# A graph attention layer with a mixture of experts: the first destination terms behind another block's softmax, flags made during the features, one scan across partitions, rows normalised on ScalarE

## The chip, the cores and the metric

The kernel runs on one core of one Trainium2 chip. The metric is device time in microseconds (us) of one execution; the median of ten runs is given. A profile is one execution recorded by the hardware profiler. The engines are TensorE (PE; its weight loads PEld), VectorE (DVE), ScalarE (ACT), GpSimd (POOL) and SyncE (SP, which here only issues DMAs). Each works through its own instructions in order.

## The reference, cut to what matters

30,000 nodes with 256 features, 510,000 edges sorted by destination, 8 relations, 4 heads of 64. A graph attention layer with a residual is followed by a feed-forward layer with a shared network and 4 experts, of which each node takes 2.

```python
# _layernorm(x) = (x - mean) / sqrt(var + 1e-5)
feat_all = jnp.einsum('ni,rhid->rnhd', inputs, conv_weights)      # inputs = _layernorm(x)
feat_src_e = feat_all[edge_type, edge_src]
feat_dst_e = feat_all[edge_type, edge_dst]
el = jnp.sum(feat_src_e * attn_l[edge_type], axis=-1)
er = jnp.sum(feat_dst_e * attn_r[edge_type], axis=-1)
e = jax.nn.leaky_relu(el + er, negative_slope=0.2)
m = jax.ops.segment_max(e, edge_dst, num_segments=N_NODES)
ex = jnp.exp(e - m[edge_dst])
alpha = ex / jax.ops.segment_sum(ex, edge_dst, num_segments=N_NODES)[edge_dst]
h = jax.ops.segment_sum(alpha[..., None] * feat_src_e, edge_dst, num_segments=N_NODES)
x = x + h.reshape(N_NODES, 256) + h_bias
x = x + ffn(_layernorm(x))     # shared + gated top 2 of 4 experts, three layers each
```

## The kernel before

**Stage 1, the features** (0 to about 1740 us). For each of 235 tiles of 128 nodes, `group` multiplies the normalised rows with all relations' weights in five groups of columns (L305), `store` writes the rows of features `feat` to memory, 1040 bytes for each node and relation: four heads of 64 and a 65th element, the source term `el`. `dest_pieces` writes the destination terms as three bf16 pieces, `erp_d`. Beside this, one step at a time (`aside`), run three generators: `edge_records`, `places` and `expert_weights`. `places` takes the edges in batches of 12 blocks, loads their records (`fetch`, tile `rcb`), and makes for each block a row of data `rk_d` of 128 partitions x `WR` words: gather indices (`WI`), the node of each edge (`WD`), marks of duplicates (`WA`), penalties of -1e30 where a new destination begins (`WP`), running minima of these from the left and from the right (`W1`: "no boundary so far", "no boundary after") and one-hot relations (`WT`). Where a generator says `yield`, its next instructions come at a later place of the feature loop. Last, `first_rows` gathers the first edge row of each block already in this stage into staging buffers (`fr`, three of them) and writes them to `stage`: the gathers are GpSimd's, the writes SP's.

**Stage 2, the blocks** (to about 6590 us). The edges are cut into 252 blocks of at most 2048 (128 partitions x `U` = 16 edges), with a 253rd of 18 a partition. Edges of a partition follow each other, so a destination's run of edges may go on from one partition to the next. The steps of block t:

- `load`: SP loads `rk`, `dr`, `erp`, `xt`. `gather`: one row from `stage` (SP), 15 rows by GpSimd's indirect DMA (L933) into a ring of four blocks (`ft`).
- `dest_select` (VectorE, L970) makes one-hot rows `ohT`; `dest_expand` (TensorE, L987, four matmuls for a quarter of the block) brings the destination terms of each edge into PSUM (`pe`, two buffers); `dest_pick` (VectorE, L998 and L1000) picks those of its relation into `e`. Four quarters each.
- `flags` (ScalarE, L951 to L955) copies the penalties to each head and the two end values into `ends`; `flags_across` (TensorE L962, ScalarE L964) turns the ends so that the 128 partitions stand in a row.
- `scores` (VectorE, L1027 to L1034) adds the gathered source terms, applies the leaky slope, and scans running maxima from the left and the right within each partition, `fb`. `turn_ends` (TensorE, L1040, L1041), `across` (VectorE, L1047 and L1048, two scans over 128 partitions), `turn_back` (TensorE, L1055, L1056) carry the maxima across partitions. `softmax` (VectorE, L1062 to L1065 and `exchange`) subtracts the maximum; `exps` (ScalarE, L1071, L1072) takes the exponential.
- `onehot` (ScalarE, L1010, L1011) makes one-hot columns of the destinations; `weigh` (VectorE, L1079) multiplies the gathered rows by the weights, and `sums` (TensorE, L1086) adds them by destination in one PSUM tile `po`; `finish` (VectorE, L1104 to L1107) divides (`den`, `ho`).
- `residual_sum` adds the residual. Four blocks make a group of 512 nodes for `Experts`: 22 steps (`spread`, `scale`, `turn`, `gates`, the layers, `last`), one taken from `todo` in each chunk.

The order on every engine is the order of the program, written out by hand: an iteration t has six chunks c, and each holds pieces of several blocks: block t's scores and softmax, t-1's weighing and sums, t+1's and t+2's destination terms, t+1's gathers, t+2's loads. In chunk 5 `softmax(t)` and `exps(t)` are followed on VectorE by `weigh(t, 0)` and `finish(t - 1)`; in chunk 0 of the next iteration come `weigh`, the first `dest_pick` and `residual_sum`. After the blocks come loops that run only where the input does not fit the blocks' limits; here they run zero times.

Of the kernel before, what the change touches and what calls it, by code (L numbers as in the profile page):

```python
# [10 lines left out]
F32 = mybir.dt.float32  # L11
# [34 lines left out]
WI, WD, WA, WP, W1, WT, WR = 0, U, 2 * U, 3 * U, 4 * U + 1, 6 * U + 3, 6 * U + 3 + U * 4  # L46
# [7 lines left out]
def kernel(  # L54
# [47 lines left out]
    stage = dram.tile([NBLK * P, H * HW], F32, name="stage")  # L102
    exc_d = dram.tile([P], F32, name="exc_d")
# [70 lines left out]
    NPEN = 3  # L174
    pens = []
    for i in range(NPEN + 1):
        f = wf.tile([P, H, U if i < NPEN else UL], F32, name=f"penf{i}")
        b = wf.tile([P, H, U if i < NPEN else UL], F32, name=f"penb{i}")
        nc.gpsimd.memset(f, -BIG)
        nc.gpsimd.memset(b, -BIG)  # L180
        pens.append((f, b))
    carry = []
    for i in range(2):
        cf = wf.tile([H, P + 1], F32, name=f"carf{i}")
        cb = wf.tile([H, P + 1], F32, name=f"carb{i}")
        nc.gpsimd.memset(cf, -BIG)
        nc.gpsimd.memset(cb, -BIG)
        carry.append((cf, cb))
# [33 lines left out]
    with ExitStack() as cx:  # L222
# [268 lines left out]
        def places(cl):  # L491
# [31 lines left out]
            yield  # L523
            done = None
            for k, (b0, n) in enumerate(batches):
# [33 lines left out]
                pen = kp.tile([P, GB, UW], F32, name="penk")[:, :n]  # L559
                nc.vector.tensor_scalar_mul(pen, rc[:, :, :, 3], -BIG)  # L560
                yield
                nc.gpsimd.tensor_copy(of[:, :, WP:WP + UW], pen)
                d16 = kp.tile([P, GB, U], I16, name="d16k")[:, :n]
                nc.gpsimd.tensor_copy(d16, rc[:, :, :U, 1])
                a1 = kp.tile([P, GB, UW], F32, name="a1k")[:, :n]
                a2 = kp.tile([P, GB, UW], F32, name="a2k")[:, :n]
# [7 lines left out]
                nc.gpsimd.tensor_copy(of[:, :, W1 + UW:W1 + 2 * UW], a2)  # L574
                yield
# [7 lines left out]
                def done(o=o, d16=d16, b0=b0, n=n):  # L583
                    nc.sync.dma_start(rk_d[b0:b0 + n].rearrange("b p w -> p b w"), o)
                    nc.sync.dma_start(dk_d[b0 * CAP:(b0 + n) * CAP].rearrange("(b p u) -> p b u", p=P, u=U), d16)
# [18 lines left out]
        def first_rows():  # L604

            n, kept = 4, []
            fp = cl.enter_context(tc.tile_pool(name="first", bufs=3))

            def keep(b0, m, fr):
                nc.sync.dma_start(stage[b0 * P:(b0 + m) * P, :].rearrange("(b p) f -> p b f", p=P), fr[:, :m])  # L610
            for b0 in range(0, NBLK, n):
                m = min(n, NBLK - b0)
                fr = fp.tile([P, n, H * HW], F32, name="fr")
                for b in range(m):
                    nc.gpsimd.indirect_dma_start(  # L615
                        out=fr[:, b], out_offset=None, in_=feat[0:BT * P * R, :],
                        in_offset=bass.IndirectOffsetOnAxis(ap=lowc[:, b0 + b:b0 + b + 1], axis=0))
                    if b == n // 2 and kept:
                        keep(*kept.pop())
                    count["sent"] += 1  # L620
                    yield
                kept.append((b0, m, fr))
            while kept:
                keep(*kept.pop(0))
# [77 lines left out]
    class Experts:  # L702
# [22 lines left out]
        def spread(self):  # L725
            self.rs = self.pool.tile([P, T], F32, name="c_rs")
            nc.scalar.activation(self.rs[:M, :self.n], self.mv[:M, :self.n, 1], AF.Sqrt, bias=eps[:M])

        def scale(self, j):
            if j == 0:  # L730
                nc.vector.reciprocal(self.rs[:M, :self.n], self.rs[:M, :self.n])
                self.xn = self.pool.tile([P, T, D], F32, name="c_xn")
            for t in range(j, min(j + 2, self.n)):
                nc.vector.tensor_scalar(self.xn[:M, t, :], self.x1[:M, t, :], self.mv[:M, t, 0:1],
                                        self.rs[:M, t:t + 1], op0=ALU.subtract, op1=ALU.mult)
# [126 lines left out]
    with ExitStack() as cx:  # L862
# [17 lines left out]
        flat = "p h u -> p (h u)"  # L880
        blk = {}

        class Block:


            def __init__(self, t):
                self.u = U if t < NBLK else UL
                self.sc = [-(-self.u * c // NCH) for c in range(NCH + 1)]
                self.dw = -(-self.u * P // 48) * 16
                self.dc = [-(-self.u * c // 4) for c in range(5)]  # L890
                at = t % RING * U
                self.ft = ring[:, at:at + self.u]
                self.own = t < NBLK
                self.pens = pens[t % NPEN if t < NBLK else NPEN]

        def load(t):
# [3 lines left out]
            if s.own:  # L900
# [7 lines left out]
                s.pen = rf[:, WP:WP + U + 1]  # L908
# [28 lines left out]
        def flags(t):  # L937


            s = blk[t]  # L940
            n = s.u
            s.penf, s.penb = s.pens
            if not s.own:
                s.pen = wk.tile([P, UL + 1], F32, name="pen", bufs=1)[:, :n + 1]
                nc.vector.tensor_scalar_mul(s.pen, s.rc[:, :, 3], -BIG)
                s.a12 = wk.tile([P, 2, UL], F32, name="a12", bufs=1)
                nc.vector.tensor_tensor_scan(s.a12[:, 0], s.pen[:, :n], s.pen[:, :n], 0.0, ALU.min, ALU.min)
                nc.vector.tensor_tensor_scan(s.a12[:, 1, ::-1], s.pen[:, n:0:-1], s.pen[:, n:0:-1], 0.0,
                                             ALU.min, ALU.min)
            mid = s.pen[:, None, 1:n].to_broadcast([P, H, n - 1])  # L950
            nc.scalar.copy(s.penf[:, :, 1:], mid)  # L951
            nc.scalar.copy(s.penb[:, :, :n - 1], mid)
            ends = wk.tile([P, 2, H], F32, name="ends")
            nc.scalar.copy(ends[:, 0, :], s.a12[:, 0, n - 1:n].to_broadcast([P, H]))
            nc.scalar.copy(ends[:, 1, :], s.a12[:, 1, 0:1].to_broadcast([P, H]))  # L955
            s.ends = ends

        def flags_across(t):
            s = blk[t]
            pn = ps_p.tile([H, 2, P], F32, name="pn", tag="sm")  # L960
            for i in range(2):
                nc.tensor.transpose(pn[:, i, :], s.ends[:, i, :], ident)  # L962
            s.through = wk.tile([H, 2, P], F32, name="through")
            nc.scalar.copy(s.through, pn)  # L964
# [26 lines left out]
        def dest_pick(t, c):  # L991

            s = blk[t]
            if c == 0:
                s.e = wk.tile([P, H * UL], F32, name="e")[:, :H * s.u].rearrange("p (h u) -> p h u", h=H)
# [28 lines left out]
        def scores(t):  # L1024

            s = blk[t]
            nc.vector.tensor_add(s.e, s.e, s.ft[:, :, :, HD].rearrange("p u h -> p h u"))  # L1027
            nc.vector.scalar_tensor_tensor(s.e, s.e, SLOPE, s.e, op0=ALU.mult, op1=ALU.max)
            exchange(s, s.e)
            s.fb = wk.tile([P, 2, H * UL], F32, name="fb")[:, :, :H * s.u].rearrange("p i (h u) -> p i h u", h=H)  # L1030
            s.f, s.b = s.fb[:, 0], s.fb[:, 1]
            e, f, b = s.e.rearrange(flat), s.f.rearrange(flat), s.b.rearrange(flat)
            nc.vector.tensor_tensor_scan(f, s.penf.rearrange(flat), e, -BIG, ALU.add, ALU.max)
            nc.vector.tensor_tensor_scan(b[:, ::-1], s.penb.rearrange(flat)[:, ::-1], e[:, ::-1], -BIG,  # L1034
                                         ALU.add, ALU.max)

        def turn_ends(t):
            s = blk[t]
            s.t1 = ps_p.tile([H, 2, P], F32, name="t1", tag="sm")
            nc.tensor.transpose(s.t1[:, 0, :], s.f[:, :, s.u - 1], ident)  # L1040
            nc.tensor.transpose(s.t1[:, 1, :], s.b[:, :, 0], ident)  # L1041

        def across(t):

            s = blk[t]
            cf, cb = carry[t % 2]
            nc.vector.tensor_tensor_scan(cf[:, 1:], s.through[:, 0, :], s.t1[:, 0, :], -BIG, ALU.add, ALU.max)  # L1047
            nc.vector.tensor_tensor_scan(cb[:, P - 1::-1], s.through[:, 1, ::-1], s.t1[:, 1, ::-1], -BIG,  # L1048
                                         ALU.add, ALU.max)

        def turn_back(t):
# [3 lines left out]
            nc.tensor.transpose(s.t2[:, 0, :], cf[:, :P], ident[:H, :H])  # L1055
            nc.tensor.transpose(s.t2[:, 1, :], cb[:, 1:], ident[:H, :H])  # L1056

        def softmax(t):
# [4 lines left out]
            nc.vector.tensor_max(c, c, s.fb)  # L1063
            nc.vector.tensor_max(s.f, c[:, 0], c[:, 1])
            nc.vector.tensor_sub(s.e, s.e, s.f)  # L1065
# [58 lines left out]
        with tc.manual_schedule():  # L1124
            for t in range(-2, NBLK + 12):
# [3 lines left out]
                for c in range(NCH):  # L1129
# [14 lines left out]
                    if c == 5:  # L1144
                        at(softmax, t)
                        at(exps, t)
                    if c < NCH - 1:
                        at(weigh, t - 1, c + 1)
                    if c < 4:
# [5 lines left out]
                    if c == 4:  # L1155
                        at(dest_select, t + 2)
# [4 lines left out]
                    if c == 5:  # L1161
                        at(weigh, t, 0)
                        at(dest_expand, t + 2, 0)
# [241 lines left out]
```

## Time and profile before

| what | us |
|---|---|
| median of 10 runs | 6654.76 (6643.41 to 6667.78) |
| profiled execution | 6660.21 |
| its span, first to last instruction | 6658.5 |
| first gather of a block | 1743.25 |
| TensorE busy, 0 to 1700 us | 1684.30 |
| TensorE, VectorE, ScalarE, GpSimd busy, 4000 to 5000 us | 879.95, 893.69, 612.94, 742.72 |
| mean granted TensorE clock, 0 to 1700 and 4000 to 5000 us | 1.00 and 0.96 of full speed |
| DMA share, 4000 to 5000 us | 0.56, 159 GB/s |

How the profile is read: a line of the groups gives the program line, the engine, the operation, `out<-in` by tile names, the partitions x elements of output and input, the count; then busy time in us and the mean of one in ns; then the idle time of that engine just before these instructions and what ended most of it. "issue" is idle time in which the profile shows nothing waited for. A line of the timeline gives the start, the duration, engine, line and operation, and in brackets the idle time before it with its releaser. An instruction that does not depend on the one before it may start some 0.08 us before that one's end is recorded, so start-to-start distances are shorter than durations.

### The profile page before, as it was taken

The numbers are of one execution on the slowest core, as the hardware profiler recorded it, in microseconds if no ns is written. First come the engines' busy times: TensorE is split into PE (matmuls) and PEld (weight loads), VectorE is DVE, ScalarE is ACT, GpSimd is POOL, SyncE is SP. The second block draws the span as 40 slices with busy tenths as digits, with TensorE's granted clock in tenths as the row PEclk, the third lists the DMA queues.
The fourth block names the chain that finished last, engine by engine and source line by source line (L and its number), as shares of the span: only waits on it lengthen the run. The fifth ranks groups of instructions, "written<-read, shape, count | busy, mean of one in ns | idle before, by whom it ended". The sixth has DMA issues, their size and how long they took to land. (4 is left out here: it accounts for less than half of the span.)

```text
span 6658.5 us, 96556 instructions
## 1 busy us (share of the span) xinstructions
PE 5998.4 (90%) x25254; PEld 3850.4 (58%) x25255; DVE 5351.3 (80%) x13882; ACT 3427.4 (51%) x9511; POOL 4070.3 (61%) x4327
## 2 busy tenths in 40 slices
PE   9999999999788888888888888888888888888888
PEld 5555555555456555565655656556656655656555
DVE  5555677644589998998899998889888888888996
ACT  2222222222365666666666666666566666566664
POOL 1111111266677777777777777777777777777773
PEclk9999999999899999999999999999999999999999
DMA  6666777799755555555555555555555555555552
GB/s 228 227 208 188 233 233 233 236 343 353 241 153 167 163 159 160 159 161 167 160 162 157 159 165 160 157 159 157 160 162 160 158 157 156 159 162 158 159 160 66
DMA packets 761457, 1209.52 MB, mean 182 GB/s; under 512 B 241638, under 2 KB 599789, under 8 KB 730685
## 3 DMA queue, kind: packets, MB, share of 16 engines
q1 hardware_dynamic: 565453, 663.56, 30.8%
q0 software_dynamic: 194400, 539.40, 29.5%
q8 instruction: 206, 3.38, 0.2%
q14 instruction: 358, 2.93, 0.1%
q10 hardware_dynamic: 1040, 0.26, 0.0%
HBM read 818.57 MB, written 384.23 MB: 181 GB/s over the span
## 5 line engine op out<-in xcount | busy, mean ns | idle before, releaser
L933 POOL DMA_INDIRECT ft<-feat,rk x3798 | 3606.6, 950 | 1227.5 <-issue 435.9
L1086 PE MATMUL po<-ft,oh 128*128 128x260 f32 x8100 | 2227.6, 410 | 154.5 <-DVE ho L1107 140.9
L1086 PEld LDWEIGHTS po<-ft,oh 128*128 128x128 f32 x8100 | 1520.5, 202 | 420.4 <-ACT ends L955 145.5
L305 PE MATMUL ps<-w,xT 128*128 128x448 f32 (+1 forms) x4700 | 1709.5, 519 | 10.1 <-DVE xT L294 8.4
L1079 DVE TENSOR_TENSOR ft<-ft,p 128x768 f32<-128x768 f32 x1518 | 1289.1, 849 | 182.2 <-ACT ft L1072 182.2
L1010 ACT ACTIVATE oh<-icol,rk 128x128 f32<-128x128 f32 x4032 | 1329.1, 390 | 0.0
L305 PEld LDWEIGHTS ps<-w,xT 128*128 128x128 f32 x4700 | 876.4, 191 | 699.0 <-issue 607.6
L307 ACT COPY fo<-ps 128x448 f32<-128x448 f32 (+1 forms) x711 | 377.9, 533 | 1081.4 <-PE ps L305 979.2
L1011 ACT ACTIVATE oh<-oh 128x384 f32<-128x384 f32 x1518 | 740.2, 488 | 48.1
L987 PEld LDWEIGHTS <-ohT 128*128 128x128 bf16 x4050 | 391.0, 158 | 403.5 <-issue 309.2
L1000 DVE TENSOR_REDUCE e<-ere 128x16 f32<-128x384 f32 (+1 forms) x1012 | 561.4, 555 | 34.7
L998 DVE TENSOR_TENSOR ere<-pe,rk 128x384 f32<-128x384 f32 x1008 | 551.1, 547 | 1.3 <-PE pe L987 1.3
L798 PE MATMUL ph<-xT,v 128*128 128x512 f32 (+1 forms) x1024 | 484.3, 596 | 1.1 <-ACT h L799 0.7
L987 PE MATMUL pe<-erp,ohT 128*128 128x96 bf16 x4050 | 434.5, 232 | 26.2 <-DVE ohT L970 20.7
L1071 ACT ACTIVATE p<-e 128x64 f32<-128x64 f32 (+1 forms) x253 | 71.1, 281 | 745.2 <-DVE e L1022 734.2
L307 DVE COPY fo<-ps 128x448 f32<-128x448 f32 (+1 forms) x464 | 242.7, 527 | 215.2 <-PE ps L305 209.6
L294 DVE COPY xT<-ptr 128x256 f32<-128x256 f32 x229 | 97.3, 425 | 370.2 <-PE ptr L292 368.0
L615 POOL DMA_INDIRECT fr<-feat,lowc x252 | 239.5, 950 | 169.1 <-DMA stage<-fr 69.7
L970 DVE TENSOR_SCALAR ohT<-dr,rowid 128x2064 bf16<-128x2064 int16 (+1 forms) x253 | 324.1, 1281 | 3.3 <-DMA feat<-fo 2.9
L274 POOL TENSOR_TENSOR xb<-xg,hb 128x1024 f32<-128x1024 f32 (+1 forms) x59 | 142.1, 2408 | 283.1 <-DMA xg<-in_x_dram 143.9
L851 PE MATMUL pf<-w,h 128*128 128x256 f32 x506 | 170.6, 420 | 145.2 <-ACT wT L844 111.8
L853 PE MATMUL pf<-v,a 128*128 128x256 f32 x1012 | 281.2, 403 | 0.0
(206 smaller groups left out, 6763.6 us busy)
## 6 DMA issues: line engine op xcount, KB each, us to landing
feat<-fo SPq DMA_DIRECT2D x234, 1040.0 KB
dr<-dk_d SPq DMA_DIRECT2D x252, 516.0 KB
ft<-feat,rk POOLq DMA_INDIRECT x3798
stage<-fr SPq DMA_DIRECT2D x63, 520.0 KB
ft<-stage SPq DMA_DIRECT2D x252, 130.0 KB
xt<-xb_d SPq DMA_DIRECT2D x253, 128.0 KB
out_dram<-og SPq DMA_DIRECT2D x253, 128.0 KB
xb_d<-xb SPq DMA_DIRECT2D x58, 512.0 KB
```

Of the source, the lines that this page charges most:

```text
L305: nc.tensor.matmul(ps, t["xT"][:, k, :], w[:, k, c0:c1], start=k == 0, stop=k == 1)
L307: eng(t["fo"][:, h0:h1, :HD], ps[:, :n].rearrange("p (a d) -> p a d", d=HD))
L798: nc.tensor.matmul(ps[:, :self.w], lhs, rhs, start=i == 0, stop=i == len(pairs) - 1)
L933: nc.gpsimd.indirect_dma_start(out=s.ft[:, u].rearrange("p h d -> p (h d)"), out_offset=None, in_=feat[:, :], in_offset=bass.IndirectOffse ...
L970: nc.vector.tensor_scalar(ohT[:, :3 * s.dw].rearrange("n (i e) -> n i e", i=3), s.dr[:, :, :s.dw], rowid[:, t:t + 1], None, op0=ALU.is_equal)
L987: nc.tensor.matmul(pe[:, u - u0].rearrange("p f r -> p (f r)"), s.ov[:, u, :], s.erp.rearrange("n h k r -> n (h k r)"), start=True, stop=True)
L998: nc.vector.tensor_mul(ere, s.pe[:, :u1 - u0], s.th[:, u0:u1, None, :].to_broadcast([P, u1 - u0, H * 3, R]))
L1000: nc.vector.tensor_reduce(s.e[:, :, u0:u1].rearrange("p h u -> p u h"), ere.rearrange("p u (h k) r -> p u h (k r)", h=H), AX.X, ALU.add)
L1010: nc.scalar.activation(s.oh[:, u, :], icol, AF.Abs, bias=s.nd[:, u:u + 1])
L1011: nc.scalar.activation(s.oh[:, u0:u1], s.oh[:, u0:u1], AF.Relu, bias=1.0, scale=-1.0)
L1079: nc.vector.tensor_mul(fc, fc, pc[:, :, None].to_broadcast([P, (u1 - u0) * H, HD]))
L1086: nc.tensor.matmul(s.po.rearrange("n h d -> n (h d)"), s.oh[:, u, :], s.ft[:, u].rearrange("p h d -> p (h d)"), start=u == 0, stop=u == s. ...
```

## The change

- **First destination terms.** In chunk 4 `dest_select(t + 2)` now stands ahead of the last `weigh`, and `dest_expand(t + 2, 0)` moves from chunk 5 into chunk 4. `dest_pick(t + 2, 0)` moves from chunk 0 of the next iteration to chunk 5, behind `softmax(t)` and `exps(t)`. `e` gets a third buffer.
- **Flags across partitions.** `places` makes the penalties per direction (`WP` is now 2 x `U` words, so `WR` grows from 163 to 178), and turns the end values of 12 blocks at once on TensorE (a transpose, and a product with `turned`, the matrix that reverses the partitions) into `thr_d`. In stage 2 `load` brings a block's 8 rows of it (`through`, three buffers); `flags` becomes one copy, and `flags_across` stays for the last block alone.
- **One scan.** Both directions stand in 8 rows, the right-hand one reversed by `turned`; `across` has one scan and a reversed copy instead of two scans. `turn_ends` and `turn_back` have as many matmuls as before, and `fb` becomes two fixed buffers with zeros between, cleared at the start.
- **Rows of the experts' layer norm.** ScalarE scales by 1/sigma and adds -mean/sigma, which one new small VectorE operation makes.
- **Stage 1.** `places` waits six steps instead of one after its first `fetch`; three of its tiles have one buffer instead of two; `first_rows` takes three rows a staging buffer instead of four.

```diff
-WI, WD, WA, WP, W1, WT, WR = 0, U, 2 * U, 3 * U, 4 * U + 1, 6 * U + 3, 6 * U + 3 + U * 4
+WI, WD, WA, WP, W1 = 0, U, 2 * U, 3 * U, 5 * U
+WT = W1 + 2 * (U + 1)
+WR = WT + U * R // 2
...
+    turned = wf.tile([P, P], F32, name="turned")
+    nc.gpsimd.memset(turned, 0.0)
+    nc.gpsimd.affine_select(out=turned, in_=turned, compare_op=ALU.not_equal, fill=1.0, base=-(P - 1),
+                            pattern=[[1, P]], channel_multiplier=1)
...
             fetch(0)
-            yield
+            for _ in range(6):
+                yield
...
-                nc.gpsimd.tensor_copy(of[:, :, WP:WP + UW], pen)
+                nc.gpsimd.memset(of[:, :, WP], -BIG)
+                nc.gpsimd.memset(of[:, :, WP + 2 * U - 1], -BIG)
+                for i in range(2):
+                    nc.gpsimd.tensor_copy(of[:, :, WP + 1 + i * (U - 1):WP + U + i * (U - 1)], pen[:, :, 1:U])
...
+                ps = pf.tile([P, 512], F32, name="ps")[:n, :2 * P]
+                nc.tensor.transpose(ps[:, :P], a1[:, :, U - 1], ident)
+                nc.tensor.matmul(ps[:, P:], a2[:, :, 1], turned, start=True, stop=True)
+                thr = kp.tile([GB, 2 * P], F32, name="thr")[:n]
+                nc.scalar.copy(thr, ps)
...
+                    nc.sync.dma_start(thr_d[b0:b0 + n].rearrange("b i p -> b (i p)"), thr)
...
-            n, kept = 4, []
+            n, kept = 3, []
...
         def scale(self, j):
+            rs, n = self.rs[:M], self.n
             if j == 0:
-                nc.vector.reciprocal(self.rs[:M, :self.n], self.rs[:M, :self.n])
+                nc.vector.reciprocal(rs[:, 0, :n], rs[:, 0, :n])
+                nc.vector.scalar_tensor_tensor(rs[:, 1, :n], self.mv[:M, :n, 0], -1.0, rs[:, 0, :n],
+                                               op0=ALU.mult, op1=ALU.mult)
                 self.xn = self.pool.tile([P, T, D], F32, name="c_xn")
-            for t in range(j, min(j + 2, self.n)):
-                nc.vector.tensor_scalar(self.xn[:M, t, :], self.x1[:M, t, :], self.mv[:M, t, 0:1],
-                                        self.rs[:M, t:t + 1], op0=ALU.subtract, op1=ALU.mult)
+            for t in range(j, min(j + 2, n)):
+                nc.scalar.activation(self.xn[:M, t, :], self.x1[:M, t, :], AF.Identity, bias=rs[:, 1, t:t + 1],
+                                     scale=rs[:, 0, t:t + 1])
...
+                s.through = lp.tile([2 * H, P], F32, name="through", bufs=3)
+                h = thr_d[t]
+                nc.sync.dma_start(s.through, bass.AP(tensor=h.tensor, offset=h.offset, ap=[[P, 2], [0, H], [1, P]]))
...
+            if s.own:
+                nc.scalar.copy(s.pens, s.pen[:, :, None, :].to_broadcast([P, 2, H, n]))
+                return
...
+        def turned_rows(name, f, b):
+
+            t = ps_p.tile([2 * H, P], F32, name=name, tag="sm")
+            nc.tensor.matmul(t, f, ident, start=True, stop=False)
+            nc.tensor.matmul(t, b, turned, start=False, stop=True)
+            return t
...
             cf, cb = carry[t % 2]
-            nc.vector.tensor_tensor_scan(cf[:, 1:], s.through[:, 0, :], s.t1[:, 0, :], -BIG, ALU.add, ALU.max)
-            nc.vector.tensor_tensor_scan(cb[:, P - 1::-1], s.through[:, 1, ::-1], s.t1[:, 1, ::-1], -BIG,
-                                         ALU.add, ALU.max)
+            nc.vector.tensor_tensor_scan(cf[:, 1:], s.through, s.t1, -BIG, ALU.add, ALU.max)
+            nc.vector.tensor_copy(cb, cf[:, P - 1::-1])
...
                     if c == 5:
                         at(softmax, t)
                         at(exps, t)
+                        at(dest_pick, t + 2, 0)
+                    if c == 4:
+                        at(dest_select, t + 2)
                     if c < NCH - 1:
                         at(weigh, t - 1, c + 1)
-                    if c < 4:
+                    if 0 < c < 4:
                         at(dest_pick, t + 1, c)
...
-                    if c == 4:
-                        at(dest_select, t + 2)
...
                     if c == 5:
                         at(weigh, t, 0)
+                    if c == 4:
                         at(dest_expand, t + 2, 0)
```

## The prediction

> **What bounds the kernel now.** I read the page, then the waits over the block stage, then each engine's timeline through one group of four blocks, and last the two ends of GpSimd's gathers. The page says little by itself:
>
> ```profile
> PE 5998.4 (90%) x25254; PEld 3850.4 (58%) x25255; DVE 5351.3 (80%) x13882; ACT 3427.4 (51%) x9511; POOL 4070.3 (61%) x4327
> ...
> L933 POOL DMA_INDIRECT ft<-feat,rk x3798 | 3606.6, 950 | 1227.5 <-issue 435.9
> ...
> L1079 DVE TENSOR_TENSOR ft<-ft,p 128x768 f32<-128x768 f32 x1518 | 1289.1, 849 | 182.2 <-ACT ft L1072 182.2
> ```
>
> TensorE looks like the bound and GpSimd (61%) like a spectator. But look at the idle time before L933: 1227.5 us over 3798 gathers, 0.32 us each. The GpSimd timeline shows what that is:
>
> ```profile
> 4057.67 0.95 POOL L933 DMA_INDIRECT ft<-feat,rk  x1 [0.30 <-issue]
> 4058.92 0.95 POOL L933 DMA_INDIRECT ft<-feat,rk  x1 [0.30 <-issue]
> 4060.17 0.95 POOL L933 DMA_INDIRECT ft<-feat,rk  x1 [0.30 <-PE t L1056]
> 4062.78 0.94 POOL L933 DMA_INDIRECT ft<-feat,rk  x1 [1.66 <-PE po L1086]
> 4064.02 0.95 POOL L933 DMA_INDIRECT ft<-feat,rk  x1 [0.30 <-issue]
> ```
>
> One gather starts every 1.25 us whatever is named as releaser: 0.95 of work and 0.30 that no engine causes. Only 4062.78 is a real wait, for a slot of the ring of gathered rows. A block issues 15 gathers, so GpSimd needs 15 x 1.25 = 18.75 us for it. Between 2500 and 6300 us 199 passes of the onehot and softmax lines fit, 3800 / 199 = 19.10 us a block. GpSimd is within 0.35 us of its floor.
>
> The other bound is VectorE, in order, nearly without gaps, with one stall a block:
>
> ```profile
> 4022.11 0.22 DVE L1022 TENSOR_REDUCE e<-m 128x4 f32<-128x64 f32 x1
> 4023.04 0.95 DVE L1079 TENSOR_TENSOR ft<-ft,p 128x768 f32<-128x768 f32 x1 [0.71 <-ACT ft L1072]
> ```
>
> VectorE ends the softmax and waits for ScalarE's exp and copy before it can weigh. That is 143.4 us over 199 blocks, 0.72 each. TensorE waits in turn for VectorE (scores, L1040: 166.4 us; `ho`, L1086: 104.9), so it has room. Today VectorE with TensorE sets 19.10; 0.35 below it GpSimd takes over.
>
> The ends of the gather chain, first and last gather, with VectorE's first and last use of gathered rows:
>
> ```profile
> 1743.25 0.94 POOL L933 DMA_INDIRECT ft<-feat,rk  x1 [18.93 <-DMA stage<-fr]
> 1760.75 0.95 POOL L933 DMA_INDIRECT ft<-feat,rk  x1 [0.30 <-issue]
> 1763.69 0.27 DVE L1027 TENSOR_TENSOR e<-e,ft 128x64 f32<-128x64 f32 x1 [10.31 <-DMA ft<-feat,rk]
> ...
> 6557.48 0.95 POOL L933 DMA_INDIRECT ft<-feat,rk  x1 [0.30 <-issue]
> 6578.01 0.28 DVE L1027 TENSOR_TENSOR e<-e,ft 128x72 f32<-128x72 f32 x1
> ```
>
> At the start VectorE waits for gathers (2.94 us after the last issue of block 0). At the end it comes 20.5 us behind them: GpSimd ran ahead and VectorE trails.
>
> **The block stage, edit by edit.** *First destination terms behind the softmax.* L998 and L1000 of block t+2 (0.55 + 0.56, 1.05 us start to start) leave the start of the next iteration and stand where VectorE stalled, so 0.72 a block goes. Exp and copy end 0.71 us after the softmax, so the pair covers them. What pays is the weighing of block t and `ho`, 1.05 - 0.72 = 0.33 later, while the next scores come 0.72 earlier. Queued behind the pair are weigh, the `den` chain and thus TensorE's next sums; TensorE does one expert step and one expansion first, and at most `ho` waits show. `dest_select` moves ahead of the last weigh, and the expansion (4 matmuls, about 0.4 us) from chunk 5 to 4; TensorE there waits for `ohT` only where it is ahead.
>
> *Normalised rows on ScalarE.* Four L734 a group go from VectorE, 0.65 us start to start for two, 1.30; one small 128x4 operation comes (as L731, 0.15 + 0.03 to 0.06): net 1.1 a group, 0.27 a block. On ScalarE an activation of 128x256 is bounded by L1010 (128x128, 390 ns) and L799 (128x512, 683); I take 0.45, 1.8 a group. It waits for VectorE's small operation after the scores; behind it stand onehot and, in chunk 5, the exp. From there to the exp ScalarE has 1.7 + 5.5 (11 one-hot columns with their second pass) + 1.2 (two `xT` copies) = 8.4 us, and VectorE 8.2 to the end of the softmax (weighs 0.86 + 0.86 + 0.6, two picks 2.1, scans 0.63, selection 1.2, softmax 2.0); the moved pair (1.05) covers the difference and the exp. TensorE gets its rows about when it does now.
>
> *One scan.* Two scans cost 0.33 + 0.31 start to start. One scan (0.40, its successor now depends on it) and a copy of 8x128 (between L731's 0.15 and L1062's 0.28; I take 0.2) come to 0.63: nothing, between -0.1 and +0.1.
>
> The Trainium skill ("SBUF — State Buffer", the section on ports shared by engines) says that an fp32 SBUF copy or tensor_scalar on VectorE can lock GpSimd out while it writes descriptors. By that rule each new copy could hold a gather back by its length, 253 x 0.2 = 50 us (an estimate), and the sum would be 6629 instead of 6579. The trace does not bear it out: around the L734 pairs at 4071.17 and 4073.73 the gathers start at 4070.27, 4071.52, 4072.78, 4074.03, on the beat.
>
> *Flags.* TensorE loses two L962 (0.46 us busy), ScalarE L954, L955 and L964 (0.19 + 0.19 + 0.35), and two copies of 128x60 (0.23 each) become one of 128x128 (0.27 as L1072 to 0.52 as L1011). SP issues one more small load a block (about 0.35 us, as its other loads). `through` has three buffers, so that load waits for `across` three blocks back; `dr`, `erp` and `xt` queue behind it on SP and are used an iteration later.
>
> VectorE's gain is thus 0.72 + 0.27 = 0.99 a block, of which TensorE hands on part: it becomes the later one in the expert chunks, where `og` already waits (78.4 us over 50 groups). I count between 0.4 and 0.95. Either way the block falls below 18.75: **GpSimd becomes the bound**, and only 0.35 a block can be kept.
>
> **The feature stage.** TensorE is busy 1684 of the first 1700 us, so what is added there counts: two matmuls for each of 21 batches (0.11 us issue each, by L292): +5, if the scans they read are done (one step earlier in program order; 0 to +1 us each if not). The five more yields shift `places` by some 18 us, past the one stall for records:
>
> ```profile
> 579.31 0.50 DVE L534 SCALAR_TENSOR_TENSOR key<-rcb,iu 128x192 f32<-128x192 int32 x1 [12.16 <-DMA rcb<-rec]
> 582.20 4.94 PE L305 MATMUL ps<-w,xT 128*128 128x448 f32 x8 [8.40 <-DVE xT L294]
> ```
>
> -8. Net -3. GpSimd's added memsets and copy (21 x 0.6) are hidden in its idle time there (it is busy 446 of 1700 us), and VectorE's three memsets of `fb` in its 10.31 us wait for the first gathers; without that cover they are under 1.
>
> *Three rows a staging buffer instead of four.* Three buffers then hold 9 rows, not 12. GpSimd already waits 67 us for staging writes and ends 18.9 us before the first block gather, which waits for the last write. A row now takes (1724 - 1313) / 252 = 1.63 us. About 14 us pass from a buffer's last gather to the landing of its write; then three buffers turn over in 14 + 3.75 us for 12 rows, 1.5 each, and afterwards 14 + 2.5 for 9, 1.83, unless smaller writes land sooner. Bounds: 0 (today's pace is set by the feature loop's order) and 252 x 0.33 = 83 us, less the 19 of slack, 64. I take 0: fewer rows in flight queue less, and SP then meets the gather sooner.
>
> **The sum**, on the profiled execution: first block gather 1743.25 - 3 = 1740; 3797 steps at the pace of the stretch in which GpSimd never waited (547 steps from 1743.25 to 2428.79: 1.2533) = 4759, so the last gather at 6499; scores of the last block 2.94 later, 6502; from there to the end as now, 6658.5 - 6578.0 = 80.5 (a tail of TensorE's expert steps; four rows on another engine change it by under 1). Span 6582, 76 less. The profiled execution took 6660.2, its span of 6658.5 and 1.7 around it; the median of the runs, 6654.76, lies 3.7 below the span, so **6579 us**. At a pace of 1.25 exactly, with the tail 3 us shorter and 8 more from the features, 6555; with 64 of staging, 6643.
>
> **The rivals.**
> (a) *VectorE's gain counts in full*, 253 x 0.95 = 240: 6415. Against it: no gather interval below 1.24 us. 4%.
> (b) *TensorE eats most of the gain*: it idles while VectorE scores, and sums after such an idle take 2.07 us for four instead of 1.11 (4071.73), the granted clock averaging 0.96 here against 1.00 in the features. The Trainium skill ("TensorE: Matmul & The Clock Gate", part 1) has the same halving after idle. With 0.1 to 0.2 a block kept, 6605 to 6630. 10%.
> (c) *Staging is late by 20 to 64*: 6600 to 6643. 12%.
> (d) *The change does not do what it says*: the expansion waits for `ohT` in chunk 4, the stall moves from exp to `pe`, and features give the rest: 6645 to 6665. 7%.
> (e) **Slower**: staging scales with the buffers, 411 x 12 / 9 = 548 us, and the blocks start 118 late; 6579 + 118 = 6697. It decides from 95 us of staging loss, 0.38 a row. For it: today 28 waits. Against it: L above is half queueing. 10%.
>
> **Chances.** Forecast 57%, a 4, b 10, c 12, d 7, e 10. About 0.2% (13 us) is what a measurement here can tell from none. Faster: forecast, a, b, c and a part of d, 82%; same 5%; slower 13% (e and the rest of d). The forecast's own range is 6555 to 6605; with b, c and part of d, 6545 to 6650.
>
> **What would show it.** Right: L1079's wait for ACT almost gone; L933 starting every 1.25 us from first to last with no `po` waits; L1027 waiting for gathers throughout; the last gather near 6499; VectorE's busy share no higher. Wrong: `fr` waits well above 67 us and the first L933 after 1760 (c, e); L933 intervals of 2 to 4 us still there, with `og` waits grown (b); L998 waiting for `pe` behind the softmax (d).

## The result and the profile after

| | before | after |
|---|---|---|
| median | 6654.1 us (6643.19 to 6667.78, 28 runs) | 6611.24 us (6609.27 to 6615.07, 8 runs) |
| ratio, 95% interval | | 0.9935 [0.9927, 0.9944] |
| profiled execution, its span | 6660.21, 6658.5 | 6601.88, 6600.2 |
| first gather of a block | 1743.25 | 1757.42 |
| last gather | 6557.48 | 6516.98 |
| mean step from gather to gather, times 15 | 19.02 | 18.80 |

The change takes 43 us off the median and 58 off the profiled span; the profiled execution of the changed kernel, 6601.88, is quicker than all its eight timed runs. The page of the changed kernel (instructions; then line, operation, count, busy us and mean ns, idle time before and its releaser):

```profile
PE 6076.4 (92%) x25827; PEld 3902.7 (59%) x25828; DVE 5253.6 (80%) x13699; ACT 3412.5 (52%) x8777; POOL 4073.3 (62%) x4382
...
L956 POOL DMA_INDIRECT ft<-feat,rk x3798 | 3603.7, 949 | 1168.4 <-issue 396.0
...
L1109 DVE TENSOR_TENSOR ft<-ft,p 128x768 f32<-128x768 f32 x1518 | 1292.6, 852 | 92.9 <-ACT ft L1102 89.4
```

GpSimd still looks like a spectator at 62%, but its idle time per gather has fallen from 0.323 to 0.308 us: only the 0.30 of its own is left. VectorE has less to do (5351 to 5254) and TensorE more (5998 to 6076, 573 instructions more). Weigh's wait for ScalarE is halved, not gone.

VectorE's waits over the blocks, 1800 to 6500 us (total, times, longest), of the changed kernel:

```profile
DVE e L1060 <- DMA ft<-feat,rk: 90.7, 64, 3.8
DVE ft L1109 <- ACT ft L1102: 88.0, 65, 2.0
DVE og L870 <- PE pf L867: 83.8, 122, 1.1
```

and of the kernel before:

```profile
DVE ft L1079 <- ACT ft L1072: 177.3, 246, 1.5
DVE og L857 <- PE pf L854: 88.0, 135, 1.6
...
DVE e L1027 <- DMA ft<-feat,rk: 11.0, 14, 2.4
```

The order is turned round. Before, weigh waited for the exp in nearly every block (246 times) and the scores hardly ever for gathered rows. Now the exp is late about once in a group of four blocks (65 times), and about as often (64 times) the scores wait for GpSimd: VectorE has come up to the gathers. The two ends of the gather chain show it too (timeline of the changed kernel):

```profile
1744.86 0.95 POOL L625 DMA_INDIRECT fr<-feat,lowc  x1 [0.30 <-issue]
...
1753.48 0.66 SPq L620 DMA_DIRECT2D stage<-fr  x1
...
1757.42 0.94 POOL L956 DMA_INDIRECT ft<-feat,rk  x1 [11.62 <-DMA stage<-fr]
...
6516.98 0.95 POOL L956 DMA_INDIRECT ft<-feat,rk  x1 [0.30 <-issue]
6519.83 0.29 DVE L1060 TENSOR_TENSOR e<-e,ft 128x72 f32<-128x72 f32 x1 [3.63 <-DMA ft<-feat,rk]
```

At the end VectorE now waits for the last gather, where before it came 20.5 us behind. At the start something is lost: the last staging gather comes at 1744.86 (before 1723.37), its write at 1753.48 (before 1740.20), and the first block gather waits for that write, 14.2 us later than before.

### The profile page after: what moved, and what is told of

It reads as the page before. It is cut to its first block, busy times and chain, and to the rows that moved or that the text cites. A ratio compares the mean times of both kernels' runs of the same rounds, so it can differ in the third digit from the quotient of the medians.

```text
span 6600.2 us, 97530 instructions
## 1 busy us (share of the span) xinstructions
PE 6076.4 (92%) x25827; PEld 3902.7 (59%) x25828; DVE 5253.6 (80%) x13699; ACT 3412.5 (52%) x8777; POOL 4073.3 (62%) x4382
## 5 line engine op out<-in xcount | busy, mean ns | idle before, releaser
L987 PE MATMUL t<-ident,fb 128*8 128x128 f32 x506 | 103.6, 288 | 187.1 <-DVE fb L1066 186.8
```

## The experiments

Theory: GpSimd's 15 gathers bound the changed kernel; the moved pick alone takes VectorE below them; the rest of the change buys nothing in the blocks; the staging of three rows costs the late start. The main rivals: staging costs nothing that lasts; several parts are needed together; TensorE or VectorE bounds the changed kernel as much as GpSimd.

The chips differed. One group of four runs came on a chip where the kernel before takes 6662 us; the others came on three chips where it takes 8363 to 8428. There the features run as ever (first gather at the same time, granted clock 1.00), but the blocks take 25.7 to 26.2 us each with 15 gathers, with a granted clock of 0.84 to 0.86. On these chips only ratios, and times in the feature stage, can be compared.

### Staging of three or four rows (8374 us chip)

```diff
-            n, kept = 4, []
+            n, kept = 3, []
```

in the kernel before, and the reverse in the changed one.

> The kernel before, with staging buffers of three rows instead of four and nothing else. If the smaller buffers are what makes the changed kernel's first block gather late (1757 us instead of 1743), the first block gather comes at 1755 to 1762 here too, the waits for staging writes (67 us before) grow, and since nothing later catches up the time is 10 to 18 us above the kernel before: 6664 to 6672. If the lateness comes from the flags or the later start of the placing, the first block gather stays at 1743 and the time within 5 us of 6654.

> The changed kernel with staging buffers of four rows again. If staging is the late step: first block gather at 1742 to 1746, gathers every 1.253 us from there to the last one, the time 10 to 15 us below the changed kernel (6611): 6596 to 6601. If the lateness has another cause: 6611, first block gather still near 1757.

The ratios: 1.000 [0.9989, 1.0011] with three rows in the kernel before, 1.0158 [1.0141, 1.0175] for the changed kernel with four. The expected times don't apply on that chip, but the feature stage does. Kernel before with three rows:

```profile
1745.98 0.95 POOL L615 DMA_INDIRECT fr<-feat,lowc  x1 [0.30 <-issue]
...
1754.48 0.98 SPq L610 DMA_DIRECT2D stage<-fr  x1
...
1758.61 0.94 POOL L933 DMA_INDIRECT ft<-feat,rk  x1 [11.69 <-DMA erp<-erp_d]
```

Changed kernel with four rows:

```profile
1725.24 0.94 POOL L625 DMA_INDIRECT fr<-feat,lowc  x1 [0.30 <-issue]
...
1741.80 0.38 SPq L620 DMA_DIRECT2D stage<-fr  x1
1744.56 0.94 POOL L956 DMA_INDIRECT ft<-feat,rk  x1 [18.38 <-ACT pens L966]
```

The start goes with the number of rows and not with the rest of the change. Over all traces: four rows 1742.4 to 1746.4, three rows 1756.2 to 1762.9. Three rows a buffer cost 13 us (1757.42 against 1744.56) in the changed kernel and 15 (1758.61 against 1743.25) in the one before.

### Fourteen gathers a block (8374 us chip, and again on the 6662 us chip)

```diff
+                nc.sync.dma_start(s.ft[:, 1].rearrange("p h d -> p (h d)"), stage[t * P:(t + 1) * P, :])
-            for u in range(1 if s.own else 0, s.u):
+            for u in range(2 if s.own else 0, s.u):
```

The kernel leaves out the gather of every partition's second row; SP puts a copy of the staged first row in its place, so the output is not the layer's.

> The kernel before with 14 gathers a block in place of 15: the second row of each partition is left out and filled with a copy of the staged first row by SP (the work on VectorE, ScalarE and TensorE stays). If VectorE with TensorE sets the pace before the change, one gather less changes little: the start and the end of the gather chain save some us, 6635 to 6655. If GpSimd already set it, the time falls by up to 252 x 1.25 = 315 us, to about 6340 or until VectorE binds.

> The changed kernel with 14 gathers a block, the second row left out in the same way. If GpSimd's gathers set the changed kernel's pace (18.80 us a block), the floor falls to 14 x 1.253 = 17.55 and the time falls until VectorE with TensorE binds, at 18.1 to 18.65 a block: 40 to 170 us below the changed kernel, 6440 to 6570. If VectorE with TensorE sets it already, less than 10 us: above 6600. How far it falls measures what the change took off VectorE and TensorE.

> The changed kernel with the second gathered row of every block taken from the staged tensor by a plain load instead of a gather (so that row holds other data; the number of operations on VectorE, ScalarE and TensorE is unchanged): 14 gathers a block. Where before takes 6654 us: theory 1 (GpSimd's gathers alone bound the changed kernel): the floor falls to 17.5 us a block and the other engines decide next, VectorE at 19.10 - 0.99 = 18.1 or TensorE a little above it, so 6430 to 6530. Theory 2 (TensorE or VectorE bound it as much as GpSimd does): 6570 to 6615, GpSimd waiting for slots of the ring 0.9 us or more a block.

On the slower chip both came out faster, 0.9732 [0.9716, 0.9748] and 0.977 [0.9754, 0.9787]. That says little of the 6654 us case: GpSimd waits for the others there, 24.8 and 24.9 us a block with 14 gathers that need 17.5.

On the usual chip the changed kernel with 14 gathers took 6539.96 us, 0.9834 [0.981, 0.9858], against 0.9933 with 15 (the run below with the rows on VectorE, on the same chip). Both theories miss: 6430 to 6530 and 6570 to 6615 were expected. GpSimd's waits, 2400 to 6400 us, with 14 gathers:

```profile
POOL ft L957 <- PE po L1117: 337.8, 803, 6.9
...
POOL ft L957 <- PE pe L1021: 82.4, 223, 7.1
POOL ft L957 <- DVE e L1034: 63.6, 40, 4.0
```

and in the changed kernel with 15:

```profile
POOL ft L956 <- PE po L1116: 269.9, 886, 0.3
POOL ft L956 <- PE pe L1020: 71.6, 235, 0.3
```

In the kernel before, in the same stretch:

```profile
POOL ft L933 <- PE po L1086: 276.2, 861, 3.4
POOL ft L933 <- PE pe L987: 69.8, 197, 3.5
...
POOL ft L933 <- DVE ft L1079: 33.0, 93, 3.7
```

The last column, the longest wait, is what counts. In the changed kernel with 15 gathers none exceeds 0.3, so GpSimd waits for nobody and is the bound. With 14 it waits up to 7 us for slots of the ring, and the pace is VectorE's and TensorE's: 14 steps of 1.3137, 18.39 us a block (18.5 between 2400 and 6400 us). So those two stand only 0.3 to 0.4 us a block below GpSimd's 18.80, if the gather left out takes nothing else off them.

### The moved pick alone (6662 us chip)

```diff
                         at(exps, t)
+                        at(dest_pick, t + 2, 0)
+                    if c == 4:
+                        at(dest_select, t + 2)
...
-                    if c < 4:
+                    if 0 < c < 4:
                         at(dest_pick, t + 1, c)
...
+                    if c == 4:
                         at(dest_expand, t + 2, 0)
```

> The kernel before with the move of the first destination pick, selection and expansion alone (three e buffers); rows stay on VectorE, the flags and the four rows a staging buffer as before. Where before takes 6654 us: theory 1 (GpSimd's gathers are the floor, 15 x 1.25 us a block, and the move alone frees 0.72 us of VectorE, more than the 0.35 that can be kept): block gathers at 1.254 to 1.257 us each from about 1743 us on, no slot waits, 6590 to 6603 us, ratio 0.990 to 0.992, thus faster than the whole change (6611), which also starts its blocks 14 us later. Theory 2 (both the move and the rows on ScalarE are needed, since TensorE hands on only part): 6615 to 6640, slot waits left. Theory 3 (the move buys nothing, it only turns the wait for ScalarE's exp into one for TensorE's pe): 6645 to 6660.

6592.61 us, 0.99 [0.9883, 0.9917]: theory 1, and below the whole change's 0.9935 [0.9927, 0.9944]. Page and last gather:

```profile
L1079 DVE TENSOR_TENSOR ft<-ft,p 128x768 f32<-128x768 f32 x1518 | 1287.0, 848 | 12.4 <-ACT ft L1072 12.1
...
6506.44 0.94 POOL L933 DMA_INDIRECT ft<-feat,rk  x1 [0.30 <-issue]
6509.26 0.29 DVE L1027 TENSOR_TENSOR e<-e,ft 128x72 f32<-128x72 f32 x1 [5.03 <-DMA ft<-feat,rk]
```

GpSimd's waits for slots, 2400 to 6400 us:

```profile
POOL ft L933 <- PE po L1086: 249.2, 818, 0.3
```

Weigh's wait for the exp is down from 182 us to 12; it is the whole change that still has 93. The first gather is at 1743.41, the mean step 1.2544 against 1.2535 in the whole change, and no wait for a slot is longer than 0.3. These few lines hold all of the gain in the blocks.

### The rows on ScalarE alone (6662 us chip)

```diff
-                nc.vector.tensor_scalar(self.xn[:M, t, :], self.x1[:M, t, :], self.mv[:M, t, 0:1],
-                                        self.rs[:M, t:t + 1], op0=ALU.subtract, op1=ALU.mult)
+                nc.scalar.activation(self.xn[:M, t, :], self.x1[:M, t, :], AF.Identity, bias=rs[:, 1, t:t + 1],
+                                     scale=rs[:, 0, t:t + 1])
```

with the small operation that makes `rs[:, 1]`, in the kernel before.

> The kernel before with the normalised rows on ScalarE alone. Where before takes 6654 us: theory 1 (VectorE's time is what separates the block from GpSimd's floor): 0.27 us a block, 253 blocks, about 65 less: 6585 to 6605, the exp wait of the weighing still near 180 us. Theory 2 (VectorE's saving is eaten by TensorE waiting for rows that come later from ScalarE): 6635 to 6660.

6664.77 us, 1.0008 [0.9998, 1.0017]: no gain, as in theory 2, but by another way than it says. VectorE's busy time does fall, by 78 us. What it waits for is ScalarE (timeline of this kernel, one block of four):

```profile
4008.03 0.22 DVE L1025 TENSOR_REDUCE e<-m 128x4 f32<-128x64 f32 x1
4009.43 1.28 ACT L1074 ACT_TABLE_LOAD   x1
4010.72 0.28 ACT L1074 ACTIVATE p<-e 128x64 f32<-128x64 f32 x1
4011.03 0.27 ACT L1075 COPY ft<-p 128x64 f32<-128x64 f32 x1
4011.34 0.95 DVE L1082 TENSOR_TENSOR ft<-ft,p 128x768 f32<-128x768 f32 x1 [3.08 <-ACT ft L1075]
```

VectorE ends its softmax at 4008.25. ScalarE, which began the rows at 4000.01, ends its one-hot columns only at 4009.40, then loads the table of exp, and weigh waits 3.08 us instead of 0.71. The load of 1.28 us comes once a group and does so in the kernel before too (63 loads at the exp in each). There, in the group at 4000 us, it is over 0.34 us before the exp can start; here it starts 1.18 us after the softmax has ended, behind the rows. Over the blocks weigh's wait for ScalarE grows from 177 to 287 us: 110 given back for the 78 gained.

### The change with rows back on VectorE (6662 us chip)

The reverse of the same diff, in the changed kernel.

> The changed kernel with the normalised rows back on VectorE (everything else of the change kept). Where before takes 6654 us: theory 1 (GpSimd is the bound and the pick alone leaves VectorE enough room): same as the changed kernel, 6605 to 6620, gathers at 1.254 to 1.257. Theory 2 (the rows on ScalarE are needed to stay under GpSimd's floor): 6625 to 6645, slot waits back.

6613.59 us, 0.9933 [0.9917, 0.995]: the same ratio as the whole change, theory 1. Weigh's wait for ScalarE falls to 31 us and nothing comes of it, since GpSimd sets the pace. Beside the pick alone, on the same chip, its gathers keep the same step (1.2548 against 1.2544) but start 19.5 us later (1762.88 against 1743.41), and its span is 17.2 us longer (6609.3 against 6592.1). So the start moves the end: what the rest of the change costs here is its late start.

### Flags, one scan and yields alone (8428 and 8363 us chips)

The changed kernel with the chunk order, the rows and the staging of the kernel before; what is left of the change has this core:

```diff
-            nc.vector.tensor_tensor_scan(cf[:, 1:], s.through[:, 0, :], s.t1[:, 0, :], -BIG, ALU.add, ALU.max)
-            nc.vector.tensor_tensor_scan(cb[:, P - 1::-1], s.through[:, 1, ::-1], s.t1[:, 1, ::-1], -BIG,
-                                         ALU.add, ALU.max)
+            nc.vector.tensor_tensor_scan(cf[:, 1:], s.through, s.t1, -BIG, ALU.add, ALU.max)
+            nc.vector.tensor_copy(cb, cf[:, P - 1::-1])
```

> The change without its moved pick, its rows on ScalarE and its staging of three rows: the flags from the features, the one scan and the six yields alone. Here VectorE with TensorE still sets the block. Where before takes 6654 us: theory 1 (the plain fp32 matmuls that turn the rows are two instructions each, so TensorE loses nothing; VectorE's scan and copy cost what two scans did; ScalarE is not late): 6640 to 6660, the 8 us stall of the features gone, 7 of it paid back for the flags there. Theory 2 (the flags free TensorE and ScalarE as the prediction counted): 6595 to 6630. Theory 3 (TensorE's longer turning between the scan and the softmax lengthens the chain of a block by 0.1 to 0.3 us): 6665 to 6720.

> The same kernel as the run before of the flags, one scan and six yields alone; there before took 8428 us, with a granted clock of 0.85 in the block stage, and this kernel 0.9% more. If before takes some 6655 here: theory 1 (TensorE loses nothing and gains nothing that counts): 6640 to 6660, ratio 0.998 to 1.001. Theory 2 (the flags free TensorE and ScalarE as the prediction counted): 6595 to 6630. Theory 3 (the chain of a block is longer by the fp32 turning matmuls, 0.1 to 0.3 us): 6665 to 6720, ratio 1.002 to 1.010. If before takes 8300 to 8500 again: the ratio of the run before, 1.007 to 1.011.

1.009 [1.0072, 1.0107] and 1.012 [1.0098, 1.0142], the second a little above the 1.007 to 1.011 expected: on those chips this part costs about 1%. Beside the first of them ran two more. The changed kernel with `n` back at 4:

> The changed kernel with four rows a staging buffer again. The traces of the runs so far start their first block gather at 1743 to 1745 us with four rows and at 1756 to 1763 with three, whatever else is changed. Where before takes 6654 us: theory 1 (that start moves the end, since GpSimd runs without a wait from there): 13 to 14 us off the changed kernel's 6611, so 6595 to 6601. Theory 2 (the later start is taken up later, by waits of VectorE and TensorE): 6608 to 6614, as the changed kernel.

1.0099 [1.008, 1.0117]: the whole change with four rows is slower there, by as much as this part of it (the same kernel had 1.0158 on the 8374 us chip). What four rows are worth in the median of a 6654 us chip wasn't measured; the start of the gathers, 1745.10, was again that of four rows.

The moved pick with one more line:

```diff
             fetch(0)
-            yield
+            for _ in range(6):
+                yield
```

> The kernel before with the moved pick and six yields ahead of the first batch of records, and nothing else of the change. The move alone took 6592.6 where before took 6661.7. Theory 1 (the 8.4 us stall of the features goes with the yields and nothing is paid for flags, and the first block gather follows the features' end): 6583 to 6588 where before takes 6660. Theory 2 (the first block gather waits for the last staging write, which the yields make later, so the features' gain is lost): 6590 to 6600.

0.9981 [0.9968, 0.9995], first gather at 1742.43: there the pick and the yields are worth 0.2% together, no more. The two theories, in times for a chip where the kernel before takes 6660 us, stay undecided. In this one trace the stall of 8.4 us is gone, but TensorE stands still for 5.9 us at 1640.4, for which the profile names no releaser, and ends its features at 1738.2, less than 1 us earlier than before. On these chips GpSimd is far from its floor (1.72 to 1.75 us a step), and a freed VectorE doesn't help.

What the flags add, from the lines of the changed kernel, TensorE's turning of rows:

```profile
L987 PE MATMUL t<-ident,fb 128*8 128x128 f32 x506 | 103.6, 288 | 187.1 <-DVE fb L1066 186.8
...
L988 PE MATMUL t<-turned,fb 128*8 128x128 f32 x506 | 103.3, 288 | 0.0
L1085 PE MATMUL t<-ident,car 8*128 8x4 f32 x506 | 97.8, 261 | 0.1
L1086 PE MATMUL t<-ident,turn 8*128 8x4 f32 x506 | 92.4, 251 | 0.0
```

and of the kernel before:

```profile
L962 PE MATMUL pn<-ident,ends 128*4 128x128 f32 x506 | 117.2, 320 | 0.0
L1041 PE MATMUL t<-ident,fb 128*4 128x128 f32 x253 | 70.7, 279 | 0.0
```

253 blocks give 506 instructions on each of the four new lines, where a transpose of `fb` gave 253: a plain product of fp32 is two instructions, a transpose one. The five lines of before (these, L1040, L1055 and L1056) have 1518 instructions and 363 us; the four of after 2024 and 397. The part takes away two transposes a block and makes the other four into products. That this is what costs 1% on the slower chips is likely but wasn't isolated there, and what the part costs where the kernel before takes 6654 us stays open: both runs came on slower chips.

## Why the prediction was right, point by point

**The bound (right).** GpSimd's 0.95 + 0.30 a gather became the bound, as foreseen. Forecast: 3797 steps at 1.2533, 4759 us; measured 1757.42 to 6516.98, 4760. Scores 2.94 after the last gather; measured 2.85. The tail 80.5; measured 80.4. Fourteen gathers confirm it: with one fewer the time falls and the bound moves on. Of the other signs named, no wait for a slot is left, but the last gather came at 6517 instead of 6499, and the scores wait for gathered rows about once a group, not throughout.

**The pick (right).** 0.72 a block from the exp wait was enough by itself to pass the 0.35 that GpSimd allows.

**The rows (the 0.27 of VectorE was about right, 78 us or 0.31 a block; the cover was not).** The sum of 8.4 us for ScalarE against 8.2 for VectorE left out the table load, 1.28, and took 0.45 for an activation that lasts 0.59 (some 0.5 start to start). The moved pair covers part of that, and weigh still waits up to 2.0 us in one block of four: 88 us in all, against 11 with the pick alone, so the exp wait isn't "almost gone". The net worth of the rows is nothing. The rows of the profile had given bounds of 0.39 and 0.68, and 0.59 lies between them. The Trainium skill ("ScalarE: Activation LUTs", section "What ACT_TABLE_LOAD costs") would have given it: 186 + 0.833 N ns, and about 93 more for each operand that is a 128x1 pointer; here with two pointers and 256 elements 585 ns (an estimate), against 589 in the trace. Its 1283 ns for a table load is the trace's number too.

**One scan (right).** `across` is 0.40 and its copy 0.24, some 0.6 start to start as the two scans were. Nor do the copies hold a gather back: the 252 steps between gathers in which one starts last 1.250 us in the mean and none over 1.262, the other steps 1.254.

**Flags (mis-sized, without effect here).** "TensorE loses two L962 (0.46 us busy)" was wrong in sign: by its lines it gains 0.13 us a block (34 us over 253), because the products count double. Between 3000 and 6000 us TensorE is busy for 2723 us in the changed kernel and for 2660 with the pick alone, at the same pace of gathers, which makes 0.4 a block. The lines of the kernel before could have told: L1086 has 8100 records for 4050 products. No cost shows where GpSimd is the bound.

**VectorE's gain of 0.99, of which 0.4 to 0.95 is handed on (borne out).** With one gather fewer the block takes 18.39 instead of 19.02, or 18.5 instead of 19.05 between 2400 and 6400 us: 0.5 to 0.6, if the gather left out takes nothing off the other engines.

**The feature stage (sign wrong, small).** The stall of 8.40 us is gone, as foreseen, but TensorE ends its features at 1741.4 us instead of 1739.0. The two matmuls of a batch are what was mis-sized (timeline of the changed kernel):

```profile
606.99 0.27 PE L580 MATMUL ps<-ident,a1k 128*12 128x128 f32 x1
607.19 0.40 PE L581 MATMUL ps<-turned,a2k 128*12 128x128 f32 x2
607.52 5.85 PE L304 MATMUL ps<-w,xT 128*128 128x448 f32 x16
```

From start to start the transpose takes 0.20 us and the product 0.33, since a product of fp32 is two instructions again: 11 us over 21 batches, where 0.11 for each of them gave 5.

**Staging (the term that was mis-sized).** "I take 0: fewer rows in flight queue less, and SP then meets the gather sooner" failed. Three rows put the last staging gather 20 us later, the last write 12 and the first block gather 13 (the changed kernel with three and with four). It was inside the bounds of 0 to 64, so rival (c) was right in kind, and the delay of 13 lies below the 20 to 64 it gave.

Together: the span is 6600.2 against 6582. Of the 18.2, 17.4 are the late start (13 staging, the rest features), 0.6 the pace. The other 14 of the 32 between 6579 and 6611.24 lie between profile and median: the profiled span of before is 4 us above its median, that of after 11 below its own. No trace shows where the timed runs spend it; with three staging rows the first gather came anywhere from 1756.2 to 1762.9, so a later start may be part of it.

So the median fell by 43 us where some 76 were forecast. It lies outside the forecast's own range of 6555 to 6605, in the stretch that was given to rival (c), and inside the 6545 to 6650 with the rivals. What made it faster was foreseen; what took back part of it was not.

**The rivals.** (a) VectorE's gain in full: no, with GpSimd's floor lowered it is 0.5 to 0.6 a block. (b) TensorE eats the gain: no, no slot waits are left, and the granted clock is 0.97. (d) The change does not do what it says: no, the pick alone gives 69 us. (e) Staging scales with the buffers: no, 13 us instead of more than 95. The chances do not add up: the forecast, (a), (b) and (c) make 83% already, more than the 82% given for faster with a part of (d).

The best version run is the kernel before with the moved pick alone, 0.99 of before. On the same chip the change with rows on VectorE, which has the whole change's ratio, took 0.3% more (6613.59 against 6592.61).

## What to carry to other kernels

An engine at 62% busy can be the bound: multiply the number of its instructions by the distance from start to start, not by their duration, and compare that with the time. Once one small edit brings the others below that floor, further edits in the same stage are worth nothing until that floor is lowered, and their side costs are what is left of them: here a late staging write. Undo each part of a bundle by itself before keeping it.

## What the hardware showed unexpectedly

Three chips ran the block stage at 25.7 to 26.2 us a block instead of 18.8 to 19.0, while VectorE's instructions lasted as long as ever (weigh 850 ns against 849) and the features ran at the same speed. The timeline of the kernel before with three staging rows shows one such place; it comes once in every group:

```profile
3067.02 1.58 PE L1086 MATMUL po<-ft,oh 128*128 128x260 f32 x6
...
3073.80 0.56 DVE L998 TENSOR_TENSOR ere<-pe,rk 128x384 f32<-128x384 f32 x1 [6.83 <-remote]
...
3079.59 0.58 ACT L744 COPY xT<-ph 128x512 f32<-128x512 f32 x1 [18.83 <-remote]
...
3080.23 2.08 PE L798 MATMUL ph<-xT,w 128*128 128x512 f32 x2 [11.62 <-issue]
```

ScalarE copies at 3079.59 what TensorE has had on record as transposed at 3067.1, and TensorE, which needs the copy, stands still for 11.6 us. VectorE stands still in the same stretch, while GpSimd's gathers go on until 3076. Then the next matmuls run at half speed: four of 128x512 take 4.2 us instead of 1.9, at a granted clock of 0.50. What holds TensorE's results back the profile doesn't name, and it wasn't found. With a gather fewer the blocks lost less (24.8 us instead of 25.7), and the kernels with the flags' part, which have more TensorE instructions, lost more (1.009 to 1.012); whether for these reasons was not tested. The change itself was not run on these chips; with four staging rows instead of three it took 1.0 and 1.6% more than the kernel before, where on the usual chips the change takes 0.65% less.
